# Transfer costs in a list schedule, and the first tiles of a second recurrence

## The chip, the cores and the metric

The kernel runs on one core of a Trainium2 chip. The metric is the device time of one execution in microseconds (us). Before the change the median of three runs is 3010.59 us (3009.65 to 3012.26). A change of about 0.2% (6 us) is what a measurement of this kernel can tell from none.

## What is computed

The input x is 2 sequences (b) of 4096 tokens with 256 channels. Layer normalisation is followed by an RWKV time mix, a recurrence along the tokens, and its result is added to x; then a second layer normalisation and two layers of local attention with a gated feed-forward follow. Cut to what matters:

```
xr, xk, xv = x * mix + shifted(x) * (1 - mix)          # one mix each
r, k, v    = xr @ W_r.T, xk @ W_k.T, xv @ W_v.T
per token: out = (e1*a + e2*v) / (e1 + e2 + EPS)       # state (a, b) runs along 4096 tokens
rwkv       = sigmoid(r) * out
normed     = group norm of rwkv over all tokens and 16 channels of a head
x          = x + normed @ W_o.T
twice:
  h = shift_token(x); q, k, v = split(h @ wqkv); q, k = rotary(l2norm(q), l2norm(k))
  x = x + local_attention(q, k, v) @ wo                # windows of 128, looking one window back
  h = layernorm(shift_token(x)); a, g = split(h @ w1 + b1)
  x = x + (a * gelu(g)) @ w2 + b2
```

The group norm needs its statistics over the whole sequence, so no window of a sequence can start before its recurrence has ended.

## The kernel before, in words

Everything is single precision. Tokens are cut into windows of 128; a window is a **row** (n = 0 to 127), four make a block of 512. The attention rows of sequence 0 go first (both layers), then those of sequence 1.

The kernel computes nothing at the point where an operation is written: `Plan` records every operation (`note`) with its engine, its dependences and a row (`plan.at(row)`), which is its priority. `cost` gives it two durations: `step`, for which it holds its engine's queue, and `time`, after which its result is there. `order` then makes a list schedule: of the operations whose inputs are known it takes, engine by engine, the one that can start first, and among those that can start at the same moment the one with the lowest row. `give` emits all operations in the order found, so the costs decide nothing but the order in which instructions stand on each engine; waits are added from the dependences. All instructions have the line of the emitting loop (L517; L511 and L513 for `scaled`), so the profile is read by the names of tiles.

For a transfer (all are issued on SP) the cost is the last branch of `cost`, and `order` adds, for SP alone, a common pipe `dma` through which the transfers pass:

```
            o.step, o.time = 60, 2000 + o.passes
...
                    dma = max(dma, t) + o.passes
                    o.end = max(t + time, dma + 2000)
```

Operations on the engine "either" (copies out of PSUM and the scaling of probabilities) go to ACT or to DVE; DVE may take one only where ACT would be free more than `LEAN` ns later (`earliest` and the test with `LEAN` in `order`).

**The recurrences.** `rec` (sequence 0) runs first, in nine chunks of 512 or 256 tokens, at rows -101 to -82; it ends in `group_norm`, which takes means (`gmv`) and deviations (`dm`) through two small matmuls and leaves a scale and an offset in `group`. `rec2` (sequence 1) runs in sixteen chunks of 256 tokens beside the attention rows of sequence 0: chunk 0 is loaded and projected at rows -1.5 and -0.5, chunk 1 at 4.5 and 5.5, chunk 2 at 7.5 and 8.5, chunk 3 at 10.5 and 11.5, and so on to about row 56. A chunk is loaded (`load`), normalised (`normed`), transposed (`transposed`), mixed and projected (`project`) and scanned (`scans`). Both recurrences have their tiles in one piece of memory, `arena`, laid out by the table `ARENA`: first the states, then for each tag one or two places. `spot(tag)` gives the next place of a tag in turn, counting from `turns[tag]`, which starts at -1; the first chunk of `rec2` so gets the first place of each pair. The places of `rec2` lie over those of `rec`, and a tile waits for the last reader of what lay there.

**An attention row.** `shift(n)` builds h from x: `down_by_one` moves the second half of the channels one token down in two transfers (112 and 15 partitions), a third transfer brings the one row for the next window, and a fourth copies the unshifted half. DVE takes the statistics of h (`st`, `mv`), POOL the power (`rs`), and the block's `transpose_h` follows. `differences(n)` does the same for v (`vr`), `transpose_p` puts one row of pB by a transfer (`pB<-last`), and `table(n)` loads a rotary table (`tab`). `rotated(n)` makes the product `qk` on DVE that the next row's first transposes on PE need.

Of the kernel before, what the change touches and what calls it, by code (L numbers as in the profile page):

```python
# [55 lines left out]

SEM = 60
OWN = {"gpsimd": 75}
LEAN = 700
SLACK = 1.06  # L60
LOAD = 1283
TURN = {"row": 195, "col": 95, "full": 199}
SETS = {AF.Exp: 1, AF.Tanh: 1, AF.Gelu: 2, AF.Ln: 3}
QUADS = 4
# [2 lines left out]
class Place:  # L67


    def __init__(self, size, psum=False):  # L70
        self.size, self.psum = size, psum
        self.reads, self.writes = [], []
        self.real = None
        self.users, self.bank = set(), None
        self.turn, self.first = 0, None
# [101 lines left out]
class Plan:  # L177
# [38 lines left out]

    def dram(self, shape, name):
        place = Place(int(np.prod(shape[1:])))
        place.real = self.dram_pool.tile([P, place.size], F32, tag=name, name=name)
        return self.view(place, 0, shape)  # L220

# [75 lines left out]
    def cost(self, o):  # L297

        views = [*o.outs, *o.ins]
        n = max([v.idx.size for v in views] or [1])  # L300
        psum = any(v.place.psum for v in views)
        inside = sum(v.idx.size == n and not v.place.psum for v in o.ins)
        o.set, o.lock, o.half, o.passes, name, hold = None, False, "full", 0, o.name, None
        if o.eng == "tensor":
            trans = name == "transpose"
            left = o.args[1]
            move = o.args[2] if len(o.args) > 2 else o.args[1]
            cols = max(move.idx.size, left.idx.size) if not trans else P
            o.step = (1 if trans else 2) * (cols / 1.2 + (2 if cols >= 256 else 3))
            if not trans and left.shape[0] <= 64:  # L310
                o.half = "row"
            elif not trans and left.idx.size <= 64:
                o.half = "col"
            if o.half != "full":
                o.step /= 2
            o.time = o.step + 150
        elif o.eng == "vector":
            d = 150 + 1.04 * n
            if name == "tensor_tensor_reduce":
                d = 240 + 1.04 * n  # L320
            elif name == "tensor_tensor_scan":
                d, o.lock = 203 + 2.1 * n, True
            elif name == "scalar_tensor_tensor":
                d, o.lock = 200 + 1.05 * n, inside > 1
            elif name == "tensor_tensor":
                o.lock = inside > 1
            elif name == "tensor_scalar":
                d, o.lock = 155 + (1.27 if psum else 0.98) * n, not psum and n > 16
            elif name == "tensor_copy" and not psum:
                d, o.lock = 230 + 0.45 * n, n > 16  # L330
            elif name == "bn_aggr":
                d = 172
            elif name == "reciprocal":
                d = 147 + 4 * n
            o.step, o.time = max(d - 85, 60), d
        elif o.eng in ("scalar", "either"):
            d = (160 if psum else 195) + 0.83 * n
            if name == "scaled":
                d = 305 + 0.76 * n
            elif name == "activation":  # L340
                o.set = SETS.get(o.args[2])
                if o.args[2] == AF.Identity:
                    d = 365 + 0.87 * n
                elif isinstance(o.kw.get("bias"), View):
                    d += 85
            o.step, o.time = d - 100, d
            if "accum_out" in o.kw:
                o.time = d + 200
        elif o.eng == "gpsimd":
            o.lock = name != "memset"  # L350
            if name == "tensor_tensor":
                d = 430 + 156 * n if ALU.pow in o.args else 140 + 2.22 * n
            elif name == "tensor_scalar":
                d = 230 + 1.12 * n
            else:
                d = (100 if name == "memset" else 187) + 0.98 * n
            o.step, o.time = d, d
            hold = d if n > 64 else 100
        else:
            v = min(views, key=lambda v: v.shape[0] * v.idx.size)  # L360
            size = 4 * v.shape[0] * v.idx.size
            rows = max(v.shape[0] if v.shape[0] > 1 else v.shape[1] for v in views)
            ways = max(k for k in range(1, 17) if rows % k == 0)
            o.passes = size / 170 if ways == 16 else size / (25 * ways)
            o.step, o.time = 60, 2000 + o.passes
        o.hold = hold or o.time


    def order(self):
# [16 lines left out]
        table, half, dma = 1, "full", 0.0  # L386
# [13 lines left out]
        def earliest(e, t, g):  # L400
            o = g[0]
            if o.lock and e in lock:
                t = max(t, lock["gpsimd" if e == "vector" else "vector"])
            need = sum(len(o.banks) for o in g)
            if need:
                have = sorted(b for b in banks if b is not None)
                if len(have) < need:
                    return None
                t = max(t, have[need - 1] + SEM)
            return t  # L410
# [8 lines left out]
        while todo:  # L419
            for e in engines:  # L420
# [4 lines left out]
                for t, g in waiting[e]:  # L425
                    s = earliest(e, t, g)
                    if e == "vector" and g[0].eng == "either" and free["scalar"] < max(t, free[e]) + LEAN:
                        continue
# [15 lines left out]
            t, g = pick[e]  # L444
            for o in g:
                if e == "tensor" and o.half != half:
                    t += TURN[o.half]
                    half = o.half
                if e == "scalar" and o.set not in (None, table):
                    t += LOAD  # L450
                    table = o.set
                for p in o.banks:
                    b = min((i for i in range(8) if banks[i] is not None), key=lambda i: banks[i])
                    p.bank, banks[b] = b, None
                    p.real = self.bank_tiles[b]
                    counts[p] = (len(p.users), 0.0)
                step, time = o.step, o.time
                if o.eng == "either" and e == "vector":
                    n = o.outs[0].idx.size
                    time = 150 + 1.04 * n if o.name == "copy" else 155 + 0.98 * n  # L460
                    step = time - 85
                    o.lock, o.hold = o.name == "scaled", time
                if o.eng == "either":
                    o.eng = e
                if e not in ("tensor", "sync"):
                    step, time = step * SLACK, time * SLACK
                o.start = t
                if e == "sync":
                    dma = max(dma, t) + o.passes
                    o.end = max(t + time, dma + 2000)  # L470
                else:
                    o.end = t + time
                if o.lock and e in lock:
                    lock[e] = t + o.hold
                t += step
                done.append(o)
                for p in o.uses:
                    c, last = counts[p]
                    counts[p] = (c - 1, max(last, o.end))
                    if c == 1:  # L480
                        banks[p.bank] = counts[p][1]
                        stale.add("tensor")
# [38 lines left out]
def kernel(ctx: ExitStack, tc: tile.TileContext, a: dict, out: bass.AP):  # L521
# [308 lines left out]
    def later_loads():  # L830
        nc.sync.dma_start(out=wot, in_=a["w_ot"])
        for i, t in enumerate((packs, backs, later)):
            nc.sync.dma_start(out=t, in_=a["c_mask"][:, i, :])
        nc.sync.dma_start(out=lnp, in_=a["p_ln"])
        nc.sync.dma_start(out=b1, in_=a["p_b1"])
        nc.sync.dma_start(out=qks, in_=a["p_qk"].partition_broadcast(P))
# [498 lines left out]
    for b, parts in enumerate(ARENA):  # L1335
        o = 0
# [26 lines left out]
    for j in (1, 2, 0):  # L1363
        rec.project(0, j, rec.split)
    rec2 = Recurrence(1, [TR] * (S // TR), TR, spots[1])
    for c in range(rec.n):
        if c + 1 < rec.n:
            plan.at(-90 + c)
            rec.ahead(c + 1, rec.split)
        plan.at(-90 + c)  # L1370
        rec.scans(c)
        plan.hold = plan.pieces[-1][0]
        if c == 0:
            later_loads()
        if 0 < c < 4:
            weights(0, ("qkv", "o", "12")[c - 1])
        plan.hold = None
# [22 lines left out]
    for n in range(NN + 6):  # L1400
        k, w = divmod(n, NW)
# [154 lines left out]
```

## Time and profile before

| what | value |
|---|---|
| median of three runs | 3010.59 us (3009.65 to 3012.26) |
| profiled execution | 3013.12 us, its span 3011.2 us, mean granted TensorE clock 0.995 |
| DMA | 182.5 MB, mean 61 GB/s; 1496 transfers issued on SP |
| PE waits with no producer late ("issue") | 758.4 us in 2916 places, weight loads waiting in the pipeline |
| DVE waiting for h (`DVE st` for `DMA h<-x`) | 68.0 us in 52 places, 2.9 at most |
| POOL waiting for the table | 166.2 us in 58 places |
| POOL waiting for h | 126.6 us in 29 places, 15.9 at most |
| SP waiting for x on DVE | 330.9 us in 132 places |

How to read it. PE is TensorE's matmuls, PEld its weight loads, DVE, ACT and POOL the vector, scalar and GpSimd engines, SP the queue that issues transfers. A group or timeline line has the engine, the operation, out<-in by the names of tiles, shapes and the number of instructions; in brackets stands how long the engine had been idle before it and what ended that. Idle time of an engine matters only where PE later waits for its result. The view of stages gives for a stretch its length, then the busy time of PE, PEld, DVE, ACT and POOL with the number of instructions, the granted TensorE clock (1.00 is full), the share of the DMA engines and GB/s. A transfer's line on SP is the time that SP needs to issue it, not its flight.

### The profile page before, as it was taken

Reading aid. Unit: us, or ns where it says so; the run is one execution under the profiler, and the core shown is the slowest. Engines: PE = TensorE matmul, PEld = TensorE weight load, DVE = VectorE, ACT = ScalarE, POOL = GpSimd, SP = SyncE. Lnnn points to the kernel's source line nnn. Section 1 sums busy time; section 2 is a strip of 40 time slices with the busy share of each in tenths; the row PEclk is TensorE's granted clock in tenths of the full one; section 3 lists DMA queues with packets and bytes.
Section 4 is the critical chain, followed back from the end, with each engine's and each line's share of the span. In section 5 each row is a group of like instructions: output and inputs, shape, how many; then the busy total and the mean of one; then the engine's idle time right before and its main releaser. Section 6 shows DMA issues by size and latency. Waiting matters only on the chain.

```text
span 3011.2 us, 48808 instructions
## 1 busy us (share of the span) xinstructions
PE 2947.5 (98%) x15500; PEld 1912.2 (64%) x15500; DVE 2218.2 (74%) x5077; ACT 2024.9 (67%) x5378; POOL 1437.8 (48%) x1705
## 2 busy tenths in 40 slices
PE   9978999999999999999999999999999999999998
PEld 4456566666666666666666666666666666666665
DVE  7888877888788888787676766667766666667663
ACT  7877786777767777676666566656666666666663
POOL 2226655445445454555544544545444545555550
PEclk9989999999999999999999999999999999999999
DMA  2322112111112121111122221111112121111110
GB/s 83 114 74 95 40 54 64 57 56 54 61 57 69 63 63 59 51 56 53 51 63 81 85 60 59 61 61 60 46 47 75 56 63 57 55 55 54 46 43 24
DMA packets 178314, 182.50 MB, mean 61 GB/s; under 512 B 27044, under 2 KB 147716, under 8 KB 177544
## 3 DMA queue, kind: packets, MB, share of 16 engines
q1 hardware_dynamic: 178056, 179.38, 19.4%
q8 instruction: 123, 2.02, 0.3%
q14 instruction: 135, 1.11, 0.1%
HBM read 79.17 MB, written 33.55 MB: 37 GB/s over the span
## 4 chain that ended last, share of the span: by engine, by line
PE 80%; DVE 9%; ACT 5%; DMA 2%; issue 1%; SPq 1%; POOL 1%; DVEq 0%; POOLq 0%; ACTq 0%
PE bank L517 80%; DVE arena L517 3%; SPq L517 1%; ACT arena L517 1%; DMA h<-x 1%; DVE bank L517 1%; ACT pr L517 1%; ACT L517 1%; DVE nmx L517 1%; DVE sq L517 1%; ACT pr L513 1%; DVE x L517 1%; DVE rn L517 0%; DVE qk L517 0%; DVE pB L517 0%
## 5 line engine op out<-in xcount | busy, mean ns | idle before, releaser
L517 PE MATMUL bank<-wqkv,xT 128*128 128x512 f32 x1536 | 722.0, 597 | 0.4 <-ACT xT L517 0.2
L517 POOL TENSOR_TENSOR t<-qk,tab 128x256 f32<-128x256 f32 x512 | 395.3, 792 | 527.2 <-ACT qk L517 408.1
L517 PE MATMUL bank<-hT,w 128*128 128x512 f32 (+1 forms) x1408 | 644.7, 594 | 0.0
L517 ACT ACTIVATE pr<-bank,nmx 128x129 f32<-128x129 f32 (+1 forms) x1024 | 364.6, 376 | 164.8 <-DVE nmx L517 158.3
L517 PEld LDWEIGHTS bank<-hT,w 128*128 128x128 f32 (+1 forms) x1408 | 258.9, 189 | 269.0 <-issue 247.6
L517 PEld LDWEIGHTS bank<-wqkv,xT 128*128 128x128 f32 x1536 | 268.0, 191 | 229.2 <-issue 219.2
L517 POOL TENSOR_TENSOR rn<-rn,mhalf 128x16 f32<-128x16 f32 x128 | 387.8, 3030 | 8.8
L513 ACT ACTIVATE pr<-pr,sums 128x129 f32<-128x129 f32 (+1 forms) x1004 | 329.4, 413 | 42.7 <-DVE pr L517 41.3
L517 DVE TENSOR_REDUCE rn<-sq 128x16 f32<-128x1024 f32 x128 | 155.6, 1215 | 209.6 <-ACT sq L517 209.6
L517 DVE COPY_PREDICATED bank<-packs,bank 128x254 f32<-128x254 int32 x496 | 186.0, 420 | 151.1 <-PE bank L517 150.7
L517 PE MATMUL bank<-w,hm 128*128 128x256 f32 x1280 | 287.3, 379 | 0.0
L517 PEld LDWEIGHTS bank<-w,hm 128*128 128x128 f32 x1280 | 241.4, 190 | 33.2 <-issue 1.3
L517 PE MATMUL bank<-wo,oT 128*128 128x256 f32 x1024 | 250.3, 387 | 0.0
L517 PE MATMUL bank<-kT,qT 64*128 64x256 f32 (+1 forms) x2048 | 246.1, 380 | 0.0
L517 PEld LDWEIGHTS bank<-wo,oT 128*128 128x128 f32 x1024 | 187.9, 190 | 68.3 <-issue 41.0
L517 ACT COPY qk<-bank 128x512 f32<-128x512 f32 x217 | 126.8, 585 | 151.5 <-PE bank L517 143.8
L517 POOL TENSOR_TENSOR dv<-vr,vt 128x512 f32<-128x512 f32 x124 | 168.7, 1360 | 124.5 <-PE bank L517 108.7
L517 PEld LDWEIGHTS bank<-mats,pr 128*128 128x128 f32 x1148 | 134.0, 135 | 136.7 <-issue 54.0
L517 ACT ACTIVATION_READ_ACCUMULATOR pr<-bank,nmx 128x1 f32 x1024 | 218.6, 214 | 0.0
L517 DVE TENSOR_TENSOR pB<-bank,backs 128x512 f32<-128x512 f32 x248 | 169.7, 684 | 66.4 <-PE bank L517 45.6
L517 PEld LDWEIGHTS bank<-kT,qT 64*128 64x128 f32 x2048 | 190.5, 187 | 31.4 <-issue 6.5
L517 POOL TENSOR_TENSOR tab<-tab,qks 128x256 f32<-128x256 f32 x128 | 119.2, 932 | 183.3 <-DMA tab<-in_c_rot_dram 166.2
(150 smaller groups left out, 5573.8 us busy)
## 6 DMA issues: line engine op xcount, KB each, us to landing
vr<-vt SPq DMA_DIRECT2D x124, 224.0 KB
tab<-in_c_rot_dram SPq DMA_DIRECT2D x128, 128.0 KB
kT<-kT SPq DMA_DIRECT2D x64, 256.0 KB
z<-zd SPq DMA_DIRECT2D x16, 512.0 KB
x<-in_x_dram SPq DMA_DIRECT2D x16, 512.0 KB
x1d<-x SPq DMA_DIRECT2D x16, 512.0 KB
x<-x1d SPq DMA_DIRECT2D x16, 512.0 KB
h<-x SPq DMA_DIRECT2D x128, 64.0 KB
```

The lines of the kernel that those rows point to most:

```text
L513: self.nc.scalar.activation(dst, src, AF.Copy, scale=scale)
L517: getattr(getattr(self.nc, o.eng), name)(*args, **kw)
```

## The change

`LEAN` goes from 700 to 1000. A transfer lands 2500 ns after its issue instead of 2000 (`LAND`), and it holds the SP queue for 370, 580 or 800 ns instead of 60: 370 where one side is not an on-chip tile (an argument in DRAM, or a DRAM tile, marked by `outer`), else 580 where its rows divide among 16 or only 1 ways, else 800. The turns of `rec2` for xT, x, k, v and r start at 0, so that its first tiles get the second place of each pair.

```diff
-LEAN = 700
+LEAN = 1000
 SLACK = 1.06
 LOAD = 1283
+LAND = 2500
@@ class Place
         self.reads, self.writes = [], []
+        self.outer = False
@@ def dram
         place = Place(int(np.prod(shape[1:])))
+        place.outer = True
@@ def cost
             o.passes = size / 170 if ways == 16 else size / (25 * ways)
-            o.step, o.time = 60, 2000 + o.passes
+            inner = len(views) == 2 and not any(v.place.outer for v in views)
+            o.step = 370 if not inner else 580 if ways in (1, 16) else 800
+            o.time = LAND + o.passes
@@ def order
                     dma = max(dma, t) + o.passes
-                    o.end = max(t + time, dma + 2000)
+                    o.end = max(t + time, dma + LAND)
@@ tile_block_kernel
     rec2 = Recurrence(1, [TR] * (S // TR), TR, spots[1])
+
+    rec2.turns = dict.fromkeys(("xT", "x", "k", "v", "r"), 0)
```

In the built programs the number of instructions on PE, POOL and SP is the same; 66 of the "either" operations go from DVE to ACT and 36 from ACT to DVE. The first 280 transposes and matmuls of PE stand in the same order.

## The prediction

> **What bounds the kernel now.** I read the page's busy row first, then the stages, then the single waits of TensorE, then the order of the built programs.
>
> ```profile
> span 3011.2 us, 48808 instructions
> PE 2947.5 (98%) x15500; PEld 1912.2 (64%) x15500; DVE 2218.2 (74%) x5077; ACT 2024.9 (67%) x5378; POOL 1437.8 (48%) x1705
> ...
> PE 80%; DVE 9%; ACT 5%; DMA 2%; issue 1%; SPq 1%; POOL 1%; DVEq 0%; POOLq 0%; ACTq 0%
> ```
>
> TensorE is the bound: idle for 3011.2 - 2947.5 = 63.7 us, and DMA and the SP queue hold 3% of the chain. The stages (us, then busy us of PE, PEld, DVE, ACT, POOL, then the granted clock) say where those 64 us lie:
>
> ```profile
> 180.00:240.00 60.00, 44.64 (x180) 35.42 (x179) 50.27 (x123) 35.59 (x58) 15.20 (x35) 0.87 0.40 130
> ...
> 1200.00:1260.00 60.00, 55.61 (x284) 37.28 (x284) 48.51 (x107) 39.60 (x114) 33.93 (x37) 0.97 0.19 57
> ...
> 2100.00:2160.00 60.00, 60.00 (x324) 37.44 (x323) 39.05 (x98) 36.98 (x106) 23.84 (x34) 1.00 0.16 49
> ```
>
> Between 1380 and 2940 us PE misses 2.9 us in 26 windows: nothing can be won there. The change can win in the handover from the first recurrence to the windows (170 to 400 us) and while the second recurrence runs beside them (to 1400 us). The longest PE waits of the latter, in order of time:
>
> ```profile
> 781.91 0.43 DVE L517 BATCH_NORM_STATS2 st<-h 128x6 f32<-128x256 f32 x1 [2.13 <-DMA h<-x]
> ...
> 784.46 0.77 PE L517 MATMUL bank<-mats,qk 128*128 128x128 f32 x5 [1.76 <-DVE qk L517]
> ```
> ```profile
> 1234.94 0.43 DVE L517 BATCH_NORM_STATS2 st<-h 128x6 f32<-128x256 f32 x1 [2.12 <-DMA h<-x]
> ...
> 1237.54 1.22 DVE L517 TENSOR_TENSOR qk<-sq,rn 128x1024 f32<-128x1024 f32 x1
> ...
> 1238.82 1.09 PE L517 MATMUL bank<-mats,qk 128*128 128x128 f32 x8 [2.99 <-DVE qk L517]
> ```
>
> PE names DVE, but DVE had stood 2.1 us at the head of its queue for a transfer of h, with the qk product that PE needs behind it. That is the error the change addresses: the list schedule thinks h is there sooner than it is.
>
> **Part 1: issue cost and landing.** A row needs four transfers of h (the range of durations of all in this phase, then one row's four on SP's timeline):
>
> ```profile
> L517 SPq DMA_DIRECT2D h<-x x175: 520/588/1548, 402.8 to 1388.4; - x175
> ```
> ```profile
> 278.54 2.71 SPq L517 DMA_DIRECT2D h<-x  x4
> ```
>
> Four issues (112, 128, 128 and 15 partitions) take 2.71 us of SP; the old plan counts 4 x 60 ns = 0.24. From issue to use the last one took 2.83 us (1232.11 to 1234.94; issue 0.82, then 2.0); the old plan counts 2000 ns plus 0.3 of passing. So it is 0.5 us early for a single transfer and about 3 us early for the last of four. No DMA, matmul or byte is added; the three added costs act through the order alone. I compared the built orders at each place where a PE wait of over 1.5 us follows a wait for a DMA:
> - 784.46: in the new order the qk product and the product ahead of it come before the statistics of h. PE's wait of 1.8 us goes (1.9 by start against start); next late is nothing, its own matmuls run to 782.7.
> - 1238.82: the qk product moves 16 places forward, ahead of the statistics and of three recurrence instructions. Its factor from POOL is there at 1233.7, so it ends near 1235, before PE runs dry (1235.8): 3.0 us.
> - 1171.70: pB's product moves ahead of a 1.21 us DVE sum; pB's row goes out 1.1 us earlier: 1.1 us of a wait of 1.65.
> - 289.02 (2.1), 2419.66 (1.9) and the end, 2970.7 to 2975.4 (4.9): the same orders on SP, ACT and PE, so they stay.
>
> [...] Here four issues (2.71) outlast one landing (2.0), so I go by the row.
>
> **The clock.** After the wait at 1238.82 the stages show
>
> ```profile
> 1240.00:1243.40 3.40, 3.40 (x12) 2.31 (x12) 3.40 (x7) 1.66 (x4) 1.08 (x1) 0.51 0.47 145
> ```
>
> 3.4 us at half clock, so 1.7 us of work lost. [...] The trace halved it all the same; I take 3.0 + 1.7 = 4.7. The waits at 784 and 1171 show no drop.
>
> Part 1: 1.9 + 4.7 + 1.1 = **7.7 us**.
>
> **Part 2: first tiles of the second recurrence.** With the turns at 0 its first xT, x, k, v, r take the second place of each pair. The last readers of its first x now lie at 141.1 us (the first recurrence's transposes of chunk 6) and no longer at 174.6:
>
> ```profile
> 174.52 0.80 SPq L517 DMA_DIRECT2D arena<-in_x_dram  x2
> ...
> 190.30 0.74 DVE L517 BATCH_NORM_STATS2 r_st<-arena 128x6 f32<-128x256 f32 x2
> ...
> 197.14 1.39 PE L517 MATMUL bank<-mats,arena 128*128 128x128 f32 x4 [6.27 <-ACT arena L517]
> ```
>
> The two loads move three SP places forward, the load of its second chunk moves three back (now issued at 141.95, then free only at 174.6; first used at 190, so hidden). Five DVE instructions (1.4 us), two of POOL and two of ACT move from 190..197 into earlier holes, and the first chunk's transposes and 24 matmuls follow chunk 8's at once. PE's idle 6.3 + 0.8 us go, with about 2.2 us of half clock: 9.3 us. But what PE meets next is the group statistics (gmv, 215.63), the end of a DVE/ACT chain of the first recurrence that the change leaves in its order; PE only waits there instead. Worth is what work is pulled ahead of row -1's QKV projections (now 238.28), which all later rows follow: 202.8 - 197.2 = 5.6 us of matmuls by the two orders (12 matmuls of its chunk 2's projections, 5.1, and 4 transposes of its chunk 4). Against it:
> - a copy that went to ACT delays chunk 8's transposes by some 1.9 us at 178; DVE catches that up, since another copy leaves it (it stood 2.4 us waiting at 187.0).
> - eight matmuls (3.4 us) now stand between gmv and dm, which followed after 2.2 us: dm 1.6 us later.
> - between the group's variance and its scale DVE had an empty queue (218.45 to 219.76, with POOL's power between). The new order puts 13 recurrence instructions there, 5.8 us by their spacing elsewhere: 4.5 us later.
>
> So row -1 comes 6.1 us later with 5.6 done: +0.5. Afterwards eight matmuls of chunk 3 and four transposes of chunk 5 (3.9 us) are pulled into rows 0 to 5, where PE waits 3.3, 2.6 and 0.9 us (299.9, 330.9, 335.4); perhaps half fills. No row shows the sum; its ends are -9 (the 9.3 us are kept) and +8 (6.1 plus DVE's further 2 us before row 0). I take 0, by the DVE row: DVE is busy 50 of 60 us here and is what work pulled forward has to pass.
>
> **Part 3: LEAN 1000.** 66 either-way instructions go from DVE to ACT, 36 back: net 30 x 0.6 = 18 us of 2218 and 2025, both under PE. Zero, between -4 and +6 (ten copies ahead of a probability PE waits for). One of them is at the end: the last rem copy joins ACT's three, 0.4 us on the chain before the last gelu.
>
> **Sum.** -7.7 + 0 + 0.4 = -7.3. The profiled execution took 3013.1 us (span 3011.2 and 1.9 around it), 2.5 above the median; -7.3 on the median of 3010.6 gives **3003**.
>
> **Rivals.** *No measurable change* (3010): the three repaired waits are the visible ones; some 1,100 of DVE's 5,000 instructions change their order, and new waits of the same size may appear where other estimates are wrong. For it: the largest group of PE waits after 240 us (14 us in 23 places) ends on ACT's probabilities, which no transfer cost touches. Against: where the second recurrence is over there is no wait to make.
> *The handover turns late* (slower, 3018): the price is DVE's queue between 218 and 300: 6.1 us for row -1, then chunk 3's differences and mixes (one 0.7 and six 0.45), two chunks' statistics (1.3 each) and the pulled scans (1.5), 7.5 us, ahead of rows 0 to 5; less the 5.6 done. 6.1 + 7.5 - 5.6 = +8, and the repairs undone by shifted order: 3018. It decides once the handover costs over 13 us with repairs whole, 6 with none. Both orders hold the same set of PE work through its 1460th operation, which now starts at 589.9 us: later than 596 means this rival.
> *Handover gained too* (2995): the 9.3 us stay with the 7.7. For it: PE has 5.6 us more done; against, the group chain.
> *The load isn't what was late*: DVE reached the statistics only at 190.3, 13 us after landing; but the early load lets it use earlier holes, so the order does change.
>
> **Chances.** Forecast 0.40 (3000 to 3008), no change 0.24, late 0.24, gained too 0.12. About 0.2% (6 us) is what a measurement can tell. Faster: 0.12 + 0.32 of the forecast + 0.03 = 0.47; same 0.24; slower 0.29. The range 2992 to 3018 leaves out the tails of the last two.
>
> **What would show it.** Right: no wait over 1 us before the qk transposes near 784 and 1238 and the clock full near 1240; DVE's waits for h (19.7 us in 15 places, 400 to 1400) halved; first chunk's transposes at about 191 to 193 and gmv within 1 us of 215.6; the 1460th operation between 586 and 594. Wrong: a new PE wait of over 3 us between 400 and 1400, or row -1's projections after 248.

## The result, and the profile after

The changed kernel takes 2999.39 us (median of 6 runs, 2997.91 to 3000.76) against 3010.40 us (6 runs, 3009.65 to 3012.26): 11.0 us less, ratio 0.9962, 95% interval 0.9950 to 0.9975. The profiled execution took 3000.22 us, its span 2998.2, so 13.0 less from span to span. The forecast was 3003, a gain of 7.3.

The page of the changed kernel, with the rows that stood first before: span, busy time, share of each engine in the chain that ended last.

```profile
span 2998.2 us, 48797 instructions
PE 2949.0 (98%) x15500; PEld 1915.1 (64%) x15500; DVE 2215.4 (74%) x5047; ACT 2037.0 (68%) x5408; POOL 1437.1 (48%) x1705
...
PE 89%; DVE 5%; ACT 3%; issue 1%; DMA 1%; POOL 0%; SPq 0%; POOLq 0%; DVEq 0%; ACTq 0%
```

The chain runs over TensorE for 89% and no longer 80%; DVE fell from 9% to 5%. The stages of the changed kernel (length, then busy us of PE, PEld, DVE, ACT, POOL, the granted clock, the DMA share, GB/s):

```profile
180.00:240.00 60.00, 43.71 (x173) 35.36 (x172) 47.43 (x114) 37.49 (x62) 16.59 (x33) 0.81 0.33 108
1200.00:1260.00 60.00, 57.80 (x326) 39.51 (x326) 52.06 (x103) 42.22 (x114) 30.81 (x34) 1.00 0.19 58
2100.00:2160.00 60.00, 60.00 (x333) 39.29 (x333) 46.48 (x110) 38.00 (x111) 29.18 (x38) 1.00 0.15 45
```

The stage at 1200 went from 55.61 busy at clock 0.97 to 57.80 at 1.00. The handover stage at 180 went the other way: 43.71 busy after 44.64, and 0.81 of the clock after 0.87.

Of the two waits for qk that the forecast named one is gone and the other nearly. DVE's timeline of the changed kernel, at the places that stood at 784 and 1238 before:

```profile
781.25 1.22 DVE L522 TENSOR_TENSOR qk<-sq,rn 128x1024 f32<-128x1024 f32 x1
782.38 0.42 DVE L522 BATCH_NORM_STATS2 st<-h 128x6 f32<-128x256 f32 x1
...
1225.94 1.75 DVE L522 TENSOR_TENSOR qk<-sq,rn 128x1024 f32<-128x1024 f32 x1
...
1228.93 0.41 DVE L522 BATCH_NORM_STATS2 st<-h 128x6 f32<-128x256 f32 x1
```

The statistics of h now stand behind the qk product, and they have no bracket: h is there when DVE comes. TensorE at the same places:

```profile
779.47 3.60 PE L522 MATMUL bank<-wqkv,xT 128*128 128x512 f32 x8
782.91 1.04 PE L522 MATMUL bank<-mats,qk 128*128 128x128 f32 x8
...
1227.74 1.09 PE L522 MATMUL bank<-mats,qk 128*128 128x128 f32 x8 [0.82 <-DVE qk L522]
```

Nothing is left of the first wait (1.76) and 0.82 of the second (2.99), with the clock at 1.00.

Where the time went is best read from the start of the same operation of TensorE in both traces, at points up to which both orders hold the same set of operations. A stage's gain is the change of that difference over the stage. (0.5 us of the first stage arise by 14 us, where TensorE's order is the same. In the trace of before the spacing of TensorE's 128x512 matmuls falls from 0.85 to 0.43 us where the granted clock turns to 1.00, at 11.25 us, in that of the changed kernel at 12.16; half of the 0.91 between is those 0.5 us. By the clock of the twelve traces below (170 to 340 us, laid back in steps of 3.41) this happens there at 12.66 to 14.10 us, whatever the edit; half of the difference from 11.25 is 0.7 to 1.4 us. So about 1 us of every entry in their first stage belongs to the start of that execution and not to the edit.)

| stage | ends before at | forecast | measured |
|---|---|---|---|
| first recurrence and handover | 664.7 (1,691st operation) | 0 | +0.6 |
| rows beside the second recurrence | 1527.8 (4,428th) | -7.7 | -11.8 |
| the rest, with the tail | 3007.6 | +0.4 | -1.8 |
| sum | | -7.3 | -13.0 |

In the middle stage TensorE's idle time went from 12.6 to 4.4 us (length less busy: 863.1 - 850.5 and 851.2 - 846.8); the other 3.7 of the 11.9 between these lengths is busy time, of which 1.7 is the half-clock stretch at 1240; the last 2.0 were not followed.

### The profile page after: what moved, and what is told of

Same layout as the page of the kernel before. It is cut to its first block, busy times and chain, and to the rows that moved or that the text cites. A ratio compares the mean times of both kernels' runs of the same rounds, so it can differ in the third digit from the quotient of the medians.

```text
span 2998.2 us, 48797 instructions
## 1 busy us (share of the span) xinstructions
PE 2949.0 (98%) x15500; PEld 1915.1 (64%) x15500; DVE 2215.4 (74%) x5047; ACT 2037.0 (68%) x5408; POOL 1437.1 (48%) x1705
## 4 chain that ended last, share of the span: by engine, by line
PE 89%; DVE 5%; ACT 3%; issue 1%; DMA 1%; POOL 0%; SPq 0%; POOLq 0%; DVEq 0%; ACTq 0%
PE bank L522 89%; DVE arena L522 1%; DVE sq L522 1%; ACT pr L522 1%; ACT arena L522 1%; ACT L522 1%; DVE bank L522 1%; DVE nmx L522 0%; ACT pr L518 0%; DVE qk L522 0%; DMA h<-x 0%; DVE x L522 0%; DVE rn L522 0%; DVE h L522 0%; ACT pT L522 0%
## 5 line engine op out<-in xcount | busy, mean ns | idle before, releaser
L522 DVE TENSOR_REDUCE rn<-sq 128x16 f32<-128x1024 f32 x128 | 155.3, 1213 | 134.4 <-ACT sq L522 134.4
L522 ACT COPY qk<-bank 128x512 f32<-128x512 f32 x231 | 134.7, 585 | 127.2 <-PE bank L522 111.6
L522 PE MATMUL bank<-pT,vt 128*64 128x128 f32 x2048 | 203.4, 279 | 0.0
```

What stands on the lines that cost most here:

```text
L522: getattr(getattr(self.nc, o.eng), name)(*args, **kw)
```

## The experiments

Each of the twelve was timed beside the kernel before on the same chip. Three chips were used, on which the kernel before took 3011.16, 3012.41 and 3012.98 us, so two kernels are compared by their differences from it. The table has the difference of the medians, its ratio with the 95% interval, the three stages of the profiled execution (us against the profiled execution of before), and DVE's waits for h between 400 and 1400 us in the view of waits. The stages are those of one execution of each kernel: their sum differs from the difference of the medians by up to 3.8 us (turns_only), and a stage is to be read with that in mind.

| kernel | us | ratio | to 665 | to 1528 | rest | DVE for h |
|---|---|---|---|---|---|---|
| before | 0 | 1 | 0 | 0 | 0 | 19.7 |
| the change | -11.0 | 0.9962 [0.9950, 0.9975] | +0.6 | -11.8 | -1.8 | 2.8 |
| turns_only | +6.6 | 1.0021 [1.0013, 1.0028] | +4.4 | +0.5 | -2.1 | 18.9 |
| lean_only | +3.9 | 1.0011 [1.0003, 1.0019] | +6.4 | -1.4 | -1.7 | 17.4 |
| slack_b | -3.8 | 0.9988 [0.9980, 0.9997] | +0.5 | -4.3 | -0.5 | 23.1 |
| land1500 | +10.9 | 1.0041 [1.0027, 1.0054] | +6.5 | -2.6 | +5.5 | 22.2 |
| costs_only | -19.6 | 0.9930 [0.9917, 0.9944] | -6.8 | -12.7 | -2.2 | 2.3 |
| land_only | -17.7 | 0.9944 [0.9931, 0.9956] | -3.9 | -12.5 | -2.0 | 9.0 |
| issue_only | -10.4 | 0.9967 [0.9956, 0.9978] | -0.4 | -9.7 | +0.4 | 6.0 |
| h_only | -11.0 | 0.9966 [0.9954, 0.9979] | -1.2 | -8.7 | -1.8 | 8.3 |
| land3000 | -8.7 | 0.9967 [0.9955, 0.9980] | +6.8 | -14.3 | -3.0 | 3.3 |
| costs_turns | -17.6 | 0.9939 [0.9926, 0.9951] | -2.1 | -13.2 | -2.2 | 3.1 |
| costs_lean | -9.5 | 0.9969 [0.9957, 0.9980] | +1.2 | -12.1 | -1.3 | 3.4 |
| lean_late | -24.8 | 0.9918 [0.9904, 0.9931] | -11.8 | -10.3 | -2.7 | 2.8 |

### The parts alone

**turns_only**, on the kernel before:

```diff
     rec2 = Recurrence(1, [TR] * (S // TR), TR, spots[1])
+
+    rec2.turns = dict.fromkeys(("xT", "x", "k", "v", "r"), 0)
```

> The kernel before with the places of the second recurrence's first tiles alone (turns at 0). Theory A, the transfer costs carry the change: 0, between -2 and +2 us against before; the first x load is readable at about 141, the first chunk's transposes come some 5 us earlier, gmv stays at 215.6, and row -1 comes out at the same time or later; the waits at 784 and 1238 stay. Theory B, the handover carries it: -7 to -10 us, all of it ahead of 335 us. Theory C, any new order moves the time: anything between -8 and +8, with new or vanished waits after 400 us where the turns touch nothing.

Measured: +6.6 us, outside theory A's range and against theory B; theory C's range holds it, but the loss lies ahead of 665 us. The waits at 784 and 1238 stay (1.76 and 3.46). The order of events was as forecast (first chunk's transposes at 191.3, gmv at 216.6), but the loss stands where the forecast had put a zero: row -1's first matmuls on z come at 226.4 for 221.8, its transposes of x at 245.3 for 237.3. TensorE's timeline of turns_only shows the new waits:

```profile
211.33 5.42 PE L517 MATMUL bank<-arena,wold 128*128 128x256 f32 x16 [2.15 <-DVE arena L517]
226.44 6.31 PE L517 MATMUL bank<-wot,z 128*128 128x256 f32 x16 [5.89 <-ACT z L517]
237.71 5.68 PE L517 MATMUL bank<-wot,z 128*128 128x256 f32 x16 [4.09 <-ACT z L517]
```

The wait of 6.3 us for the first chunk is gone, and TensorE waits twice for z, the next thing that waits for the group norm; the kernel before waits for z once, 1.50 us.

**lean_only**, on the kernel before:

```diff
-LEAN = 700
+LEAN = 1000
```

> The kernel before with LEAN 1000 alone. Theory A: within 2 us of before, since DVE and ACT both stand beside a full TensorE, and the waits at 784 and 1238 stay. Theory B: the same. Theory C (any new order moves the time): 3 to 8 us either way, by waits that appear or vanish at places that have to do with no copy.

Measured: +3.9 us. A and B, which cost it at nothing, miss; theory C's 3 to 8 us hold it. The waits at 784 and 1238 stay (1.53 and 3.38). The loss again lies ahead of 665 us (+6.4).

**costs_only**, on the kernel before (nothing of LEAN or the turns):

```diff
+LAND = 2500
...
-            o.step, o.time = 60, 2000 + o.passes
+            inner = len(views) == 2 and not any(v.place.outer for v in views)
+            o.step = 370 if not inner else 580 if ways in (1, 16) else 800
+            o.time = LAND + o.passes
...
-                    o.end = max(t + time, dma + 2000)
+                    o.end = max(t + time, dma + LAND)
```

> The kernel before with the three transfer costs (issue time, landing time, the pipe) and neither LEAN nor the turns. Theory A: -8 to -13 us; no TensorE wait over 1 us before the qk transposes near 784 and 1238, and the clock full near 1240. Theory B (handover): -2 to -4 us, since the repairs are partly paid back by new waits. Theory C: anything between -8 and +8 us.

Measured: -19.6 us, more than any theory gave. The wait at 784 is gone, and 1.36 us are left at 1238 (theory A had allowed no more than 1). The transfer costs are worth nearly twice the whole change; the other two parts take 8.6 back.

**costs_turns**, on the changed kernel:

```diff
-LEAN = 1000
+LEAN = 700
```

> The changed kernel with LEAN back at 700. Theory A: within 2 us of the changed kernel (about -11 us against before), and equal to the sum of the two single parts within 3 us. Theory C: parts don't add; over 4 us away from the sum.

Measured: -17.6 us. It isn't within 2 us of the changed kernel, and it is 4.6 away from the sum of the single parts (-19.6 + 6.6 = -13.0). With LEAN 1000 on top the changed kernel has -11.0: LEAN costs 6.6 us here (the two intervals only just meet, at 0.995).

**costs_lean**, on the changed kernel:

```diff
-    rec2.turns = dict.fromkeys(("xT", "x", "k", "v", "r"), 0)
```

> The changed kernel without the turns: new costs and LEAN 1000. If LEAN and the turns are prices that add: -19.6 + 4 to 6 for LEAN, so -14 to -16 us against before. If the parts don't add (each order has its own luck): anywhere between -5 and -22, with LEAN's loss gone or doubled.

Measured: -9.5. LEAN costs 10.1 us on the costs alone, 6.6 on costs with turns, 3.9 alone. The turns cost 6.6 alone, and nothing that can be told on the costs (-19.6 and -17.6) or where LEAN is 1000 already (-9.5 and -11.0): in both pairs the intervals overlap. So neither has a price of its own: what LEAN and the turns do depends on the order that they meet, and by the stages most of it is done in the first.

### Which of the costs

**land_only** and **issue_only**, on the kernel before. First land_only:

```diff
+LAND = 2500
...
-            o.step, o.time = 60, 2000 + o.passes
+            o.step = 60
+            o.time = LAND + o.passes
...
-                    o.end = max(t + time, dma + 2000)
+                    o.end = max(t + time, dma + LAND)
```

> The kernel before with the landing time of 2500 alone; a transfer still holds SP for 60. The three costs together gave -19.6 us. Theory A (the error is the summed issue time of the four transfers of h, 2.7 us against 0.24): a 0.5 us later landing can't show it, so -2 to -5 us, and the waits before the qk transposes near 784 and 1238 stay. Theory B (a later landing of each single transfer is enough to put the qk product ahead): -15 us or better, and both waits go. Theory C, any new order moves the time: between -8 and +8, at places that have to do with no transfer.

issue_only has the other half:

```diff
+LAND = 2000
...
-            o.step, o.time = 60, 2000 + o.passes
+            inner = len(views) == 2 and not any(v.place.outer for v in views)
+            o.step = 370 if not inner else 580 if ways in (1, 16) else 800
+            o.time = LAND + o.passes
```

> The kernel before with the issue times of 370, 580 and 800 alone; landing stays 2000. Theory A: nearly all of the -19.6 us, -14 to -19, and the waits near 784 and 1238 go. Theory B: -2 to -6. Theory C: between -8 and +8.

Measured: -17.7, in theory B's range, and -10.4, between the ranges of A and B. The theory of the forecast, that the summed issue time of four transfers is the error that matters, falls: 0.5 us of later landing is enough for -12.5 in the middle stage, and the wait at 784 goes. Issue time alone gives -9.7 there and leaves 0.42 us of that wait, so it is neither needed nor worth nothing. Each halves DVE's waits for h or better by itself; together they leave 2.3 us. The view of DVE's waits between 400 and 1400 us (us in total, times, longest) for land_only, and then for issue_only:

```profile
DVE st L522 <- DMA h<-x: 9.0, 11, 2.0
```
```profile
DVE st L522 <- DMA h<-x: 6.0, 5, 2.1
```

In both a wait before the qk transposes near 1238 stays, but shorter (1.85 and 1.25) and without the loss of clock: the eight projections behind it take 1.90 us in both, as the eight at 1233.93 did before, where the clock was 1.00.

**h_only**, on costs_only: the new costs for the transfers into h alone.

```diff
-            o.time = LAND + o.passes
+            h = any(v.place in (self.places.get("h_0"), self.places.get("h_1")) for v in o.outs)
+            if not h:
+                o.step, o.time = 60, 2000 + o.passes
+            else:
+                o.time = LAND + o.passes
...
-                    o.end = max(t + time, dma + LAND)
+                    o.end = max(t + time, dma + o.time - o.passes)
```

> The kernel before with the new costs for the transfers into the two h tiles of the attention rows alone (700 or so of the 1496); all others keep 60 and 2000. Theory A: the part after the handover (about -15 of the -19.6 us, after 660) is whole and the handover part (-6.8 before 665) is mostly gone: -12 to -17. Rival: the loads of x and of the tables (370 each) and the pB rows carry it: -5 or less.

Measured: -11.0, one short of theory A's range and far from its rival. The handover's gain is mostly gone (-1.2), as expected; of the middle stage's 12.7 the transfers of h carry 8.7. What carries the other 4.0 wasn't separated; it is no more than a shuffled order moves (slack_b, below, has -4.3), so it may have no cause in transfers.

**land1500** and **land3000**: land_only with `LAND` at 1500 and at 3000.

> The kernel before with a landing time of 1500 in the place of 2000: the suspected error doubled, in the other direction. So far every kernel with any of the transfer costs gained 9 to 13 us between 665 and 1528 us, and those with LEAN or the turns alone none (-1.4 and +0.5). Theory A (the stage waits for transfers that the order believes landed): more and longer waits for h there, slower by 5 to 15 us in that stage. Rival (2000 is just an unlucky value, and any other landing time gives an order that gains there): -5 or better in that stage.

> The kernel before with a landing time of 3000. Theory A: the repairs between 665 and 1528 stay whole (-10 to -14 in that stage, the waits near 784 and 1238 gone), since a transfer counted too late costs only cover that DVE has. The handover, where orders scatter by 6 us either way, decides the total: 2990 to 3003. Rival (a counted landing beyond the real one pushes work behind the transfer that PE needs): the stage gives back 5 us or more.

Measured: land3000 keeps the whole middle stage (-14.3) and loses 6.8 in the handover, 3004.29 in all, just beyond the range. land1500 is slower by 10.9, but not where theory A put it: the middle stage is at -2.6, and both waits, at 784 and at 1238, are gone there as well. The loss is in the handover (+6.5) and after 1528 us (+5.5), where TensorE waits 4.4 us for probabilities and 4.1 for pB's row. So a single wait that vanishes proves nothing: it goes in an order that counts transfers worse, too. What holds over all kernels is the sum. Without a transfer cost raised the middle stage is at +0.5, -1.4, -4.3 and -2.6, and DVE waits 17.4 to 23.1 us for h; with one, it is between -8.7 and -14.3, and DVE waits 2.3 to 9.0.

**slack_b**, on the kernel before, a control:

```diff
-SLACK = 1.06
+SLACK = 1.065
```

> Control: the kernel before with the factor on the durations of DVE, ACT and POOL at 1.065 and not 1.06, which changes the order at some 3,400 places of PE and 4,500 of DVE and has nothing to do with transfers. Theory A with a scattered handover: up to 6 us either way before 665 us, and less than 3 us from 665 to 1528, with the waits for h still there. Theory C (any new order repairs the stage): -5 or better from 665 to 1528.

Measured: -3.8, with -4.3 in the middle stage, between the two ranges. DVE still waits for h there:

```profile
DVE st L517 <- DMA h<-x: 23.1, 18, 3.2
```

So an order shuffled for another reason can win 4 us, and does so without shortening the waits for h. Gains of 9 to 14 us in that stage were reached only where those waits fell by half or more.

### LEAN, and a version that beats both

**lean_late**, on costs_only:

```diff
-LEAN = 700
+LEAN = 1000
...
-                    if e == "vector" and g[0].eng == "either" and free["scalar"] < max(t, free[e]) + LEAN:
+                    if e == "vector" and g[0].eng == "either" and free["scalar"] < max(t, free[e]) + (LEAN if g[0].at[0] > -2 else 700):
```

> The kernel with the three transfer costs and no turns, with LEAN 1000 from the second recurrence on only; the first recurrence keeps 700. With LEAN 1000 throughout this kernel took 3002.95, without it 2991.52. Theory L (LEAN's price is one copy and one scaling of chunk 8 on ACT behind a sum of the first recurrence: 854 starts at 178.7 and not at 164.4): the early part is whole again, -6 at 190 us, and the total 2990 to 2994. Rival (LEAN makes ACT the late engine in rows 0 to 8): 2998 to 3004 with the early part at -6 and given back before 340.

ACT's timeline in costs_only shows what is at stake: the last two scalings and the last copy of chunk 8 (the second of the pair at 163.97).

```profile
162.51 1.08 ACT L522 ACTIVATE arena<-arena,r_nb,r_rs 128x256 f32<-128x256 f32 x2
163.50 0.58 ACT L522 ACTIVATE x<-bank 128x512 f32<-128x512 f32 x1
163.97 1.06 ACT L522 COPY arena<-bank 128x512 f32<-128x512 f32 x2
```

The same engine in costs_lean, with LEAN 1000 from the start: the last scaling at 177.21 and that copy at 178.74.

```profile
175.99 1.32 ACT L522 ACTIVATE x<-x,mwu 128x512 f32<-128x512 f32 x2
177.21 0.59 ACT L522 ACTIVATE arena<-arena,r_nb,r_rs 128x256 f32<-128x256 f32 x1
177.70 0.62 ACT L522 ACTIVATE sq<-x 128x512 f32<-128x512 f32 x1
178.22 0.62 ACT L522 ACTIVATE qk<-x 128x512 f32<-128x512 f32 x1
178.74 0.57 ACT L522 COPY arena<-bank 128x512 f32<-128x512 f32 x1
```

That copy (854 in the expectation) stands 14 us later, and TensorE waits for chunk 8 at 177.9 and again at 179.4. With LEAN kept at 700 for the first recurrence the order is that of costs_only through the 426th operation of TensorE, and the copy is early. Measured: 2988.15 us, -24.8, below the range of theory L and against its rival. lean_late beats the kernel before and the changed one; its interval (0.9904 to 0.9931) doesn't meet that of the change. It does meet that of costs_only (0.9917 to 0.9944), so LEAN 1000 in the rows is shown to be no loss, and not to be a gain. TensorE of lean_late runs as in costs_only, within 0.1 us, up to 298 us. Of the 12.5 us between the spans of it and of costs_lean, 6.2 are there when row -1's QKV projections start (236.25 and 242.40), and all by 663 us. That the price is paid in the first recurrence is so shown; that this one copy is all of it is not, since every copy and scaling there keeps LEAN 700.

## Why the prediction was right, and where not

**The total is right in part by luck.** The wait that part 1 names, DVE standing at h with TensorE's next product behind it, is what the costs remove, and this part is shown. But the costs alone are worth 19.6 us where part 1 had 7.7, and LEAN and the turns, put at 0.4 and 0, take 8.6 back. Two errors of opposite sign bring the sum near.

**The sum of part 1 (-7.7) was right in kind and too small.** The middle stage gave 11.8. The three named places gave 1.9 at 784 (forecast 1.9), 1.8 around 1171 (1.1) and 2.7 around 1238 (4.7; a new wait of 0.8 stands there, and an operation at 1252 is 1.1 later): 6.4 of 7.7. The term that was missing is every place under 1.5 us, which the comparison of orders left out: -3.0 between 785 and 909 (among it a wait of 1.18 for qk; 1.1 of the 3.0 is given back by 1055), and -2.3 between 1205 and 1213 where three waits for probabilities (0.91, 0.25 and 0.25) are gone. The forecast had called those waits ones that no transfer cost touches. In the middle stage TensorE's waits for probabilities fell from 3.6 us to 1.4. DVE's waits for h were to be halved; they fell to a seventh.

**"The same orders on SP, ACT and PE, so they stay" failed at 2419.66.** The orders of these three are the same; DVE's isn't. DVE in the kernel before:

```profile
2415.32 0.43 DVE L517 BATCH_NORM_STATS2 st<-h 128x6 f32<-128x256 f32 x1 [2.88 <-DMA h<-x]
2415.66 0.68 DVE L517 TENSOR_TENSOR sq<-qk,tab 128x512 f32<-128x512 f32 x1
2416.25 0.68 DVE L517 TENSOR_TENSOR pB<-bank,backs 128x512 f32<-128x512 f32 x1
```

and in the changed kernel:

```profile
2400.91 1.28 DVE L522 TENSOR_TENSOR sq<-qk,tab 128x512 f32<-128x512 f32 x2
2402.11 0.42 DVE L522 BATCH_NORM_STATS2 st<-h 128x6 f32<-128x256 f32 x1
2402.83 0.69 DVE L522 TENSOR_TENSOR pB<-bank,backs 128x512 f32<-128x512 f32 x1 [0.30 <-ACT pT L522]
```

The wait for h of 2.88 us stood ahead of pB's product, which ACT's copies and the transfer of pB's row need; TensorE's 1.72 us wait for that row is gone, 1.9 us in all. The wait at 289.02 went too, though other waits of that stage took its place; the one at the end stayed (4.73 before and after). The tail lost 0.9, forecast 0.4.

**The issue cost was given too much weight.** The forecast went by the row, and the row was right (2.71 us for four issues). But landing alone is worth 17.7 and issue alone 10.4, where the row would have had issue worth nearly all. Here the list schedule didn't pay back the size of an error; either cost was enough to put one instruction behind another.

**Part 2 had its steps right, but its zero holds for the stage by luck, and not for the part.** First chunk's transposes came at 191.3 (forecast 191 to 193), gmv at 214.7, dm 1.7 later (forecast 1.6), the 1,460th operation at 593.4 (586 to 594), row -1's transposes of x at 244.7 for 237.3, 7.4 later. Its QKV projections, from which the forecast counted, start at 247.03 for 238.28: 8.8 later where 6.1 was forecast, short of the 248 that was to mean it wrong. The named reason is in DVE's timeline. Before, the two steps from variance to scale of the group norm:

```profile
218.45 0.16 DVE L517 COPY group<-bank 128x2 f32<-128x2 f32 x1 [0.61 <-PE bank L517]
219.76 0.16 DVE L517 TENSOR_TENSOR group<-group,vec 128x2 f32<-128x2 f32 x1 [1.15 <-POOL group L517]
```

and in the changed kernel, with the pulled instructions of the second recurrence between them:

```profile
219.83 0.16 DVE L522 COPY group<-bank 128x2 f32<-128x2 f32 x1 [0.96 <-PE bank L522]
219.91 1.26 DVE L522 SCALAR_TENSOR_TENSOR arena<-arena,vec 128x256 f32<-128x256 f32 x3
221.17 1.39 DVE L522 TENSOR_TENSOR_SCAN arena<-arena,s 128x256 f32<-128x256 f32 x2
...
225.20 0.15 DVE L522 TENSOR_TENSOR group<-group,vec 128x2 f32<-128x2 f32 x1
```

1.31 us became 5.37: DVE works through all of it without a pause, where it had stood idle for 1.15 us. TensorE waits for z behind it. Before:

```profile
221.83 4.14 PE L517 MATMUL bank<-wot,z 128*128 128x256 f32 x16
231.37 3.99 PE L517 MATMUL bank<-wot,z 128*128 128x256 f32 x16 [1.50 <-ACT z L517]
```

and in the changed kernel:

```profile
227.57 5.21 PE L522 MATMUL bank<-wot,z 128*128 128x256 f32 x16 [5.93 <-ACT z L522]
237.49 5.37 PE L522 MATMUL bank<-wot,z 128*128 128x256 f32 x16 [3.44 <-ACT z L522]
```

By row 3 the delay is 8.6 us, and by 665 us it is 0.6: the pulled work is paid back. But the runs show three terms behind that +0.6, which the forecast did not have: the costs give -6.8 there, the turns take about 4.7 (costs_turns less costs_only), LEAN about 2.7 (the change less costs_turns). That they nearly cancel is chance. In costs_only chunk 8's copy comes early and gmv follows at 213.11 for 215.63, 2.5 us; the rest of its 6.8 wasn't followed. The third of the waits that the forecast hoped to half fill (0.9 at 335.4) is none: TensorE works from 330.85 to 338 with one pause of 0.28, and its matmuls are slow there: the clock is 0.50 from 332.10 to 335.51.

**Part 3's zero failed.** LEAN costs 6.6 us in the change, just beyond the +6 allowed. The forecast took 18 us of moved work as hidden under TensorE and named the copy at 178 us as one that DVE catches up. lean_late shows the first recurrence to be the place; what its copies and scalings wait behind counts, not their sum.

**The rivals.** *No measurable change* rested on waits that fill again: they didn't, at least in these stages. *The handover turns late* described turns_only (+4.4 to 665 us), but in the change its deciding sign, the 1,460th operation later than 596, didn't come. *Gained too* and *the load isn't what was late* aren't seen: the idle 6.3 us ahead of the first chunk went, and the two waits for z came.

What stays open: whether transfers beside those of h carry the other 4 us of the middle stage, and how much of the handover's scatter (-11.8 to +6.8 over all kernels) has causes that can be planned for.

## What to carry to other kernels

Put measured issue and landing times into a list schedule first, and judge them by the sum of the waits that they address over a whole stage and against a shuffled order, not by one wait that is gone. Change one knob at a time: here a good part was worth 20 us and two companions, each free by the sum of busy times, took nearly 9 of them back. In a serial chain (statistics, power, scale) work that is pulled into an engine's hole makes the chain later by what is longer than the hole: here 4.1 us (1.31 became 5.37). An idle engine there is cover and no waste.

## What the hardware showed

**What a wait of TensorE cost in clock depended on where it fell.** In the traces of the two kernels fourteen stretches at half clock end within the trace: eight are 3.41 us long, five 6.83 and one 10.24. Each starts a whole number of 3.41 us after the first full clock, which came at 11.25 us in the kernel before and at 12.16 in the changed one. Stretches of the kernel before at that spacing (length, busy us of PE, PEld, DVE, ACT, POOL, granted clock, DMA share, GB/s):

```profile
294.55:297.97 3.42, 2.22 (x9) 0.97 (x7) 2.05 (x8) 2.99 (x13) 3.42 (x3) 1.00 0.18 51
297.97:301.38 3.41, 1.48 (x14) 1.46 (x15) 2.23 (x6) 2.87 (x7) 0.72 (x2) 1.00 0.06 14
328.69:332.10 3.41, 0.97 (x6) 0.68 (x7) 3.41 (x8) 2.85 (x8) 1.59 (x2) 1.00 0.13 34
332.10:335.51 3.41, 3.41 (x12) 2.38 (x11) 3.41 (x8) 2.23 (x5) 1.00 (x2) 0.50 0.01 1
1236.64:1240.05 3.41, 1.24 (x10) 1.21 (x11) 3.38 (x5) 1.20 (x2) 3.41 (x3) 1.00 0.01 1
1240.05:1243.46 3.41, 3.41 (x12) 2.32 (x12) 3.41 (x7) 1.67 (x4) 1.03 (x1) 0.50 0.49 149
```

The wait of 3.13 us before 299.90 is the longest of the three and cost no clock: it lies across the edge of two such stretches and leaves 2.22 and 1.48 us busy, and the clock stays at 1.00 until 332.10. Waits of 2.46 and 2.99 us that fall (all but 0.3 of the first) into one stretch leave 0.97 and 1.24 busy, and the next 3.41 us were granted 0.50. Laid over both whole traces, some 1,730 stretches have the full clock. All twelve of them with 1.26 us busy or less were followed by one at 0.50; of the five with 1.48 to 1.69 two were (1.50 and 1.67, in the changed kernel); of those with 1.91 or more none was. Of the stretches at 0.50, the fourteen with at least 3.05 us busy were followed by one at 1.00, the seven with 2.53 or less by another at 0.50.

**Idle time turned into slow time.** Between 165 and 340 us the changed kernel's TensorE waits less and runs slower. Before:

```profile
165.00:340.00 175.00, 146.87 (x743) 105.47 (x741) 145.01 (x334) 123.25 (x282) 84.69 (x118) 0.94 0.25 80
```

and in the changed kernel:

```profile
165.00:340.00 175.00, 147.83 (x698) 105.09 (x697) 143.00 (x339) 120.55 (x276) 84.74 (x118) 0.90 0.25 80
```

One us more of busy time did 45 fewer matmuls (of mixed shapes). The stretches of 3.41 us granted 0.50 in it are 6 before and 10 after. TensorE is busy for 17.1 and 27.4 us of them, and half of that is lost, 8.6 and 13.7 us of work: 5.1 us that no view of waits shows. It isn't one execution's chance alone: the mean clock is 0.993 or 0.994 in all six runs of the changed kernel, and 0.994 to 0.996 in those of the kernel before that were timed beside the twelve.
